# First group of a cross-attention and expert kernel: second scores in the common PSUM banks, beside the next unit's first scores

## The chip, the cores and the metric

The kernel runs on one core of a Trainium2 chip. The metric is device time in microseconds. Engines are named as in the profile: PE (TensorE, matrix products), PEld (its weight loads), DVE (VectorE), ACT (ScalarE), POOL (GpSimd) and SP (SyncE, which issues most loads). PSUM, where PE puts its results, has eight banks of 512 fp32 columns by 128 partitions.

## What is computed

Sixteen images, 100 tokens of width 256 each, attend to 361 context rows with 16 heads of width 16; then a mixture of 16 experts with 64 slots each works on the result. All in fp32.

```python
x = x + xattn(layernorm(x), ctx, mask)     # q, k, v projections, softmax(q k / 4 + mask) v, projection wo
# the experts, per image
xn = layernorm(x1) * norm_g + norm_b
logits   = xn @ se.T                       # 1024 slots, se a layer norm of slot_embeds
dispatch = softmax(logits, over tokens)    # slots = dispatch.T @ xn
combine  = softmax(logits, over slots)
eout     = (gelu(slots @ Wg + bg) * (slots @ Wu + bu)) @ Wd + bd     # per expert
out      = x1 + combine @ eout
```

## The kernel before

The images go in groups of 2, 2, 4, 4 and 4. A group's attention, its dispatch (slots of the experts) and its experts follow each other, and while the experts of one group run, the attention of the next is woven in between. Nothing of that is decided on the chip: while the program is built, a planner (the loop at L1354) keeps a clock for each engine (`Clock`, L64) with an estimated cost for every step, and picks the next step among generators (`Task`, L106). A step says when it can run, how many of four PSUM banks it takes, and what it needs of PE, DVE and ACT. The order in which steps are picked is each engine's order of instructions; on the chip an engine runs its queue in that order, and each instruction waits for its inputs and for its place in memory. Until the first expert step (`begun`), the planner puts *warm products* (L1337, products with the identity that nothing reads) where its clock says that PE would be idle.

PSUM is split in two: four banks are one fixed tile `at` (`at_all`), the other four are a pool that everything else takes in turn (`mm_tile`).

Attention runs in *units*: one image `b`, and four of its heads `cb` (class `Unit`, L769), each head on 32 of the 128 partitions. A unit does, all in `at`:

- `maxima` (L781): first scores, four products of 100 x 361, one bank each (L785), and their negated row maxima by DVE into `mxp` (L790);
- `queries` (L796): the maxima transposed by PE into free columns of `at` (L799) and added to the queries by DVE (L801), so that the second scores come out with the maximum taken off;
- `exponentials` (L805): second scores, transposed, twelve products of 121 x 100 (L810), and one exponential of 1200 columns by ACT (L818);
- `values` (L824): twelve products with the values (L833) into a pool bank, copied by ACT to `cxs` (L842).

`units` (L862) orders them for a group: first scores of a unit, values of the unit before, queries, second scores and exponentials. The first group is images 0 and 1, eight units; unit 4 is the first of image 1.

The side work of the first group: `key_work` (L570: transposed context `c_t` L584, keys `k_ps` L613 with DVE L634 and ACT L639, mask rows by SP L653, values `v_ps` L673 with copies L684 or L687), `query_work` (L491: layer norm with DVE, a power by POOL L447, z L504, `x_t` L519, queries `q_ps` L538 with DVE L548 and ACT L551; L563 adds bo's row to x by POOL), `slot_work` (L451: statistics of `slot_embeds`, its power by POOL, ACT L467, `se_t` L476 and ACT L482), `parameter_work` (L397), `bo_work` (L413: `bo_ps` L423, L426), `out_work` (L701: for each unit a shuffle L713 and a reciprocal L714 by DVE and a product by POOL L717; then `o_ps` L726, the sum L734, the second layer norm, z L747, `xn_t` L752 and ACT L758) and `early_work`. Keys and queries of images 2 and 3, the second group, are side work here too. Then come `dispatch_quarter` (L927: logits L942, DVE L967, ACT L972, `d_t` L1020, slots `sl` L1032) and the experts (L1284, L1244).

While the first group runs, the order of preference among the kinds of side work is a list (`kinds`, L1388), and a step is let in only if by its needs it doesn't keep the next step of the units waiting (`fits`, L1415 on; `lead` holds the steps that must not wait).

Of the kernel before, what the change touches and what calls it, by code (L numbers as in the profile page):

```python
# [33 lines left out]
F32 = mybir.dt.float32  # L34
AF = mybir.ActivationFunctionType
# [9 lines left out]
KC = 120  # L45
# [10 lines left out]
SLACK = 0.6  # L56
BACKLOG = 2.5
ASIDE = ("out_work", "query_work", "key_work")
MASK_DMA = 5.0
COLD = 7.0  # L60
HOP = 0.12
# [68 lines left out]
def xattn_ffn_kernel(  # L130
# [360 lines left out]
    def query_work(b, n=2):  # L491

        g = group_of[b]
        i0 = b - starts[g]
        yield x_t[g], 0, (0.0, 0.65 * n, 0.0)
        mv4 = two.tile([N, 2, 2], F32, tag="mv4", name="mv4")
        for i in range(n):
            ck.run("DVE", stats(accs[g][:, i0 + i, :], N, mv4[:, i, :]), x_t[g])
        r4 = rstd(mv4[:, :n, 1], N, n)
        t = ck.run("POOL", 0.7, ck.run("DVE", 0.15))  # L500
        yield t, 0, (0.0, 0.45 * n, 0.0)
        z4 = const.tile([N, 2, D], F32, tag="z4", name="z4")
        for i in range(n):
            nc.vector.tensor_scalar(  # L504
                z4[:, i, :],
                accs[g][:, i0 + i, :],
                mv4[:, i, 0:1],
                r4[:N, i : i + 1],
                ALU.subtract,
                ALU.mult,  # L510
            )
            t = ck.run("DVE", 0.35, t)
        z_done.add(b)
        yield t, 1, (0.2 * n, 0.0, 0.25 * n)
        xT = const.tile([P, KD, 2 * N], F32, tag="xT", name="xT")
        ps = mm_tile("x_t")
        for kd in range(KD):
            for i in range(n):
                nc.tensor.transpose(  # L519
                    ps[:, (n * kd + i) * N : (n * kd + i + 1) * N],  # L520
                    z4[:, i, kd * P : (kd + 1) * P],
                    ident[:N, :N],
                )
        nc.scalar.copy(
            xT[:, :, : n * N], ps[:, : KD * n * N].rearrange("p (k n) -> p k n", k=KD)
        )
        t = ck.copy(200 * n, ck.run("PE", 0.2 * n, t, ck.bank()))
        ck.free(t)
        yield t, 1, (0.7 * n, 0.5 * n, 0.5 * n)
        if b % 2 == 0:  # L530
            qp = two.tile([P, KD, 2, 2 * N], F32, tag="qp", name="qp")
        else:
            qp = qps[b - 1][0]
        cols = slice(b % 2 * N, (b % 2 + n) * N)
        ps = mm_tile("q_ps")
        for oc in range(KD):
            for kd in range(KD):
                nc.tensor.matmul(  # L538
                    ps[:, oc * n * N : (oc + 1) * n * N],
                    lhsT=w_sb["wq"][:, kd, oc * P : (oc + 1) * P],  # L540
                    rhs=xT[:, kd, : n * N],
                    start=kd == 0,
                    stop=kd == KD - 1,
                )
        t = max(ck.pe(400 * n, t, ck.bank()), par_t[0] if par_t[0] < NEVER else 10.5)
        for oc in range(KD):
            src = ps[:, oc * n * N : (oc + 1) * n * N]
            nc.vector.tensor_scalar(  # L548
                qp[:, oc, 0, cols], src, hm[:, 0:1], qb[:, oc, 0:1], ALU.mult, ALU.add
            )  # L550
            nc.scalar.activation(  # L551
                qp[:, oc, 1, cols], src, AF.Identity, bias=qb[:, oc, 1:2], scale=hm[:, 1:2]
            )
            first = ck.psum_dve(100 * n, t)
            t = ck.copy(100 * n, first)
            if b == oc == 0:
                qps[b] = (qp, first)
        ck.free(t)
        for i in range(n):
            qps.setdefault(b + i, (qp, t))  # L560
        yield (lambda: bo_t[0]), 0, (0.0, 0.0, 0.0)
        a = accs[g][:, i0 : i0 + n, :]
        nc.gpsimd.tensor_tensor(a, a, bo_bc[:N].unsqueeze(1).to_broadcast([N, n, D]), ALU.add)  # L563
        t = ck.run("POOL", 0.55 * n)
        for i in range(n):
            with_bo[b + i] = t
# [202 lines left out]
    class Unit:  # L769
# [35 lines left out]
        def exponentials(self):  # L805
# [15 lines left out]
            if self.cb == 3:  # L821
                live.discard(self.b)

        def values(self):  # L824
            if self.cb == 0:
                live_cxs.add(self.b)
# [18 lines left out]
            cx_t[self.b, self.cb] = t  # L845

    free_t = [0.0]
    phase = [""]
    cx_t = {}
    group_of = {b: g for g, n in enumerate(GROUPS) for b in range(starts[g], starts[g] + n)}  # L850
# [6 lines left out]
    def values_ready(u):  # L857
        if u.b not in values_t or (u.cb == 0 and len(live_cxs) == 2):
            return NEVER
        return max(u.t, values_t[u.b])  # L860

    def units(g):  # L862
        last = None

# [6 lines left out]
                fill.append(Task(key_work(u.b + 2), ck))  # L871

        group = range(starts[g], starts[g] + GROUPS[g])
        for b in group:
            for cb in range(4):
                yield (
                    lambda: max(keys[b, cb][1], qps[b][1]) if (b, cb) in keys and b in qps else NEVER
                ), 0, (0.0, 0.0, 0.0)
                yield free_t[0], 0, (0.8, 1.7, 0.0)
                u = Unit(b, cb)  # L880
                u.maxima()
                if cb == 0 and b % 2 == 1 and b + 1 in group:
                    fill.append(Task(query_work(b + 1), ck))
                if last:
                    lt = last
                    yield (lambda: values_ready(lt)), 1, (0.7, 0.0, 0.3)
                    finish(last)
                yield u.t, 0, (0.15, 0.25, 0.0)
                u.queries()
                yield u.t, 0, (0.85, 0.0, 1.2)  # L890
                u.exponentials()
                last = u
# [461 lines left out]
    while streams["experts"]:  # L1354
# [29 lines left out]
        if waiting:  # L1384
            units_first = dispatches[:WINDOW] + units_first
            side = sorted(fill, key=lambda t: t.kind != "out_work")
            if group == 1 and 0 in qps:
                kinds = (  # L1388
                    "early_work",
                    "bo_work",  # L1390
                    "query_work",
                    "parameter_work",
                    "slot_work",
                    "out_work",
                    "key_work",
                )
                side = sorted(
                    fill,
                    key=lambda t: kinds.index(t.kind) if t.kind in kinds else len(kinds),
                )  # L1400
# [14 lines left out]
        if not begun:  # L1415
# [7 lines left out]
            else:  # L1423
                lead = [
                    i
                    for i, t in enumerate(tasks)
                    if t.kind in ("out_work", "all_experts") or t in dispatches[:1]
                ] if group > 1 else []
            soonest = min((ready[i] for i in lead), default=NEVER)
            by_keys = any(t.kind in ("key_work", "later_keys") and r <= now for t, r in zip(tasks, ready))  # L1430
            for i, t in enumerate(tasks):
# [6 lines left out]
                late = 0.15 + SLACK * pe  # L1438
                if not first_units:
                    fits = max(end, vector, scalar) <= soonest + late  # L1440
                elif phase[0] == "max":
                    fits = max(end, vector) <= soonest + late and scalar <= soonest + late + 1.2
                elif phase[0] != "queries":
# [10 lines left out]
            if ready[-1] <= now:  # L1454
                ready[:-1] = [NEVER] * (len(ready) - 1)
        first = next((i for i, r in enumerate(ready) if r <= now), None)
        if first is None:
            first = min(range(len(ready)), key=lambda i: ready[i])
            assert ready[first] < NEVER
            if not begun and now + 0.2 < ready[first] and phase[0] != "queries":  # L1460
                warm_up()
                continue
        task = tasks[first]
        begun = begun or task is streams["experts"]
        task.step()
        if task.done:
# [63 lines left out]
```

## Time and profile before

| | us |
|---|---|
| median of 3 runs | 1177.96 (1177.79 to 1178.29) |
| span of the profiled execution | 1178.0 |
| PE busy in the span | 1160.2 |
| first unit's first scores | 11.73 |
| last product of the first group's units ends | 64.5 |
| first dispatch logits | 73.0 |
| first expert product | 82.0 |

The span goes from the first to the last instruction of one profiled execution, whose own time with what lies around the span was 1179.8 us. In a timeline line the first two columns are the start and the duration in us, then engine, line, operation, what is written and read, how many in the row, and in brackets how long the engine sat idle before it and what ended that. PE runs an fp32 product as two instructions, so twelve products are a row of 24, and a PE row's duration holds some pipeline time that the next row overlaps; the chain of waits gives such rows without it.

### The profile page before, as it was taken

What the parts mean: (1) busy time and instruction counts of PE and PEld (TensorE: products, weight loads), DVE (VectorE), ACT (ScalarE), POOL (GpSimd) and SP (SyncE); (2) the same over time, 40 slices, a digit from 0 to 9 for tenths busy, and PEclk for the clock granted to TensorE, in tenths of its full rate; (3) what the DMA queues carried; (4) which work ended last, traced back from release to release, by engine and by line L of the source; (5) the groups of instructions that cost most, each with busy time, mean ns of one, the idle gap of its engine ahead of it and who ended that gap; (6) DMA issues with size and microseconds to landing.
All of it is one profiled execution on the core that took longest, in us unless ns stands there. A gap on an engine that the chain in (4) does not pass through costs nothing.

```text
span 1178.0 us, 24309 instructions
## 1 busy us (share of the span) xinstructions
PE 1160.2 (98%) x9825; PEld 899.1 (76%) x9825; DVE 632.8 (54%) x1559; ACT 539.8 (46%) x1112; POOL 150.9 (13%) x255
## 2 busy tenths in 40 slices
PE   8899999999999999999999999999999999999998
PEld 6587778787787777767777776787878878777876
DVE  5755545565654565655386767656543455442222
ACT  3557554664544667434454634646312336314110
POOL 3110301013000131300010010304000003002000
PEclk9999999999999999999999999999999999999999
DMA  4412656543566603212341321333344343345431
GB/s 134 136 38 97 233 174 203 162 145 116 154 201 220 188 11 90 83 58 100 113 105 53 111 91 38 98 126 112 112 158 137 118 148 126 112 129 163 138 131 55
DMA packets 138588, 144.85 MB, mean 123 GB/s; under 512 B 45050, under 2 KB 97228, under 8 KB 138476
## 3 DMA queue, kind: packets, MB, share of 16 engines
q1 hardware_dynamic: 137258, 141.50, 38.6%
q8 instruction: 78, 1.28, 0.4%
q0 software_dynamic: 496, 1.12, 0.3%
q10 hardware_dynamic: 722, 0.67, 0.2%
q14 instruction: 34, 0.28, 0.1%
HBM read 141.60 MB, written 1.66 MB: 122 GB/s over the span
## 4 chain that ended last, share of the span: by engine, by line
PE 94%; DVE 2%; ACT 2%; DMA 1%; issue 1%; POOL 0%; SPq 0%; ACTq 0%; DVEq 0%; POOLq 0%
PE dn L1244 19%; PE gp L1284 19%; PE up L1284 19%; PE sl L1032 5%; PE po L1162 5%; PE at L810 4%; PE at L785 4%; PE lg L942 3%; PE cx L833 3%; PE v_ps L673 3%; PE k_ps L613 3%; PE at L1337 1%; PE o_ps L726 1%; DVE mxp L790 1%; DMA w_all<-in_L_ffn_Wd_dram 1%; PE q_ps L538 1%
## 5 line engine op out<-in xcount | busy, mean ns | idle before, releaser
L1284 PE MATMUL gp<-ring,w_all 128*128 128x256 f32 (+1 forms) x1280 | 247.8, 340 | 1.3 <-ACT lg_all L963 1.3
L1284 PE MATMUL up<-ring,w_all 128*128 128x256 f32 (+1 forms) x1280 | 246.6, 340 | 0.0
L1300 DVE SCALAR_TENSOR_TENSOR hT<-up,parT,ge 128x256 f32<-128x256 f32 (+1 forms) x320 | 119.6, 423 | 233.3 <-PE up L1284 163.0
L1244 PE MATMUL dn<-w_all,hT 128*64 128x256 f32 x2048 | 232.9, 382 | 1.4 <-DMA w_all<-in_L_ffn_Wd_dram 1.3
L1295 ACT ACTIVATE ge<-gp,parT 128x256 f32<-128x256 f32 (+1 forms) x320 | 116.8, 429 | 249.5 <-PE gp L1284 245.3
L1284 PEld LDWEIGHTS gp<-ring,w_all 128*128 128x128 f32 x1280 | 203.4, 191 | 27.5 <-issue 4.9
L1284 PEld LDWEIGHTS up<-ring,w_all 128*128 128x128 f32 x1280 | 203.7, 191 | 21.4 <-issue 1.2
L1244 PEld LDWEIGHTS dn<-w_all,hT 128*64 128x64 f32 x2048 | 142.7, 137 | 79.8 <-issue 8.3
L790 DVE TENSOR_REDUCE mxp<-at 100x4 f32<-100x1444 f32 x64 | 106.2, 1660 | 30.7 <-PE at L785 30.0
L1253 DVE TENSOR_TENSOR ring<-dn,bd_bc 128x512 f32<-128x512 f32 x64 | 44.2, 691 | 136.3 <-PE dn L1244 136.2
L818 ACT ACTIVATE aT<-at 121x1200 f32<-121x1200 f32 x64 | 74.9, 1170 | 64.3 <-PE at L810 60.9
L1295 ACT ACT_TABLE_LOAD x60 | 77.0, 1283 | 26.7 <-PE gp L1284 24.3
L1012 DVE STREAM_TRANSPOSE disp<-d_ex 32x128 f32<-32x128 f32 x256 | 77.4, 302 | 4.5
L717 POOL TENSOR_TENSOR cxs<-cxs,rs 128x100 f32<-128x100 f32 x63 | 24.8, 396 | 390.7 <-DVE rs L714 363.3
L1047 ACT ACTIVATE ring<-sl,parT 128x256 f32<-128x256 f32 x64 | 32.6, 561 | 67.9 <-PE sl L1032 67.9
L1032 PE MATMUL sl<-disp,xn 100*128 100x256 f32 x256 | 63.4, 388 | 0.2 <-ACT disp L1025 0.2
L1162 PE MATMUL po<-ring,lg_all 128*100 128x256 f32 x256 | 60.5, 383 | 0.4 <-DVE ring L1253 0.2
L997 POOL TENSOR_TENSOR d_ex<-d_ex,d_sm 128x400 f32<-128x400 f32 x28 | 23.8, 852 | 267.7 <-DVE d_sm L994 240.6
L810 PEld LDWEIGHTS at<-q,kT 32*121 32x121 f32 x1344 | 40.6, 180 | 19.9 <-issue 8.8
L1032 PEld LDWEIGHTS sl<-disp,xn 100*128 100x128 f32 x256 | 46.4, 190 | 10.3 <-issue 2.6
L810 PE MATMUL at<-q,kT 32*121 32x100 f32 x1344 | 49.9, 277 | 3.4 <-DVE q L801 3.3
L818 ACT ACT_TABLE_LOAD x36 | 46.2, 1283 | 14.2 <-PE at L810 6.2
(152 smaller groups left out, 1268.4 us busy)
## 6 DMA issues: line engine op xcount, KB each, us to landing
w_all<-in_L_ffn_Wg_dram SPq DMA_DIRECT2D x80, 512.0 KB
w_all<-in_L_ffn_Wu_dram SPq DMA_DIRECT2D x80, 512.0 KB
w_all<-in_L_ffn_Wd_dram SPq DMA_DIRECT2D x80, 512.0 KB
bd_bc<-in_L_ffn_bd_dram SPq DMA_DIRECT2D x80, 64.0 KB
c_sb<-in_ctx_dram SPq DMA_DIRECT2D x96, 44.0 KB
acc<-in_x_dram SPq DMA_DIRECT2D x7, 200.0 KB
out_dram<-acc SPq DMA_DIRECT2D x7, 200.0 KB
ring<-n_L_ffn_slot_embeds_dram POOLq DMA_DIRECT2D x1, 1024.0 KB, 6.6
```

Source lines behind the costliest of these rows:

```text
L785: nc.tensor.matmul(self.at[:N, r, :S2], lhsT=self.q[rows], rhs=self.k[rows], start=True, stop=True)
L790: nc.vector.tensor_reduce(mxv[:, :, m : m + 1], self.at[:N, :, :S2], AX.X, ALU.max, negate=True)
L810: nc.tensor.matmul(self.at[: KC + 1, r, c * N : (c + 1) * N], lhsT=self.k[rows, c * KC : c * KC + KC + 1], rhs=self.q2[rows], start=True, ...
L818: nc.scalar.activation(self.aT[: KC + 1], self.at[: KC + 1, :, : 3 * N], AF.Exp)
L1012: nc.vector.transpose(dst[toks, :, :, a, :], src[32 * a : 32 * a + 32, :, :, toks])
L1032: nc.tensor.matmul(sl[:, kd * 256 : (kd + 1) * 256], lhsT=xns[g][:, b0 + i, kd * P : (kd + 1) * P], rhs=disp[:, i, :], start=True, stop=True,)
L1162: nc.tensor.matmul(pos[i][:N, :D], lhsT=lg_all[:, slot, 2 * c + i, :], rhs=eouts_of(g, q)[:, c, 2 * p + i, :], start=c == 0, stop=c == 1,)
L1244: nc.tensor.matmul(dn[S * x : S * x + S, i * D : (i + 1) * D], lhsT=hts[x][fc // FB][0].rearrange("p (f b s) -> p f b s", f=FB, s=S)[:, fc ...
L1253: nc.vector.tensor_tensor(eouts_of(g, q)[:, j // 2, 2 * half : 2 * half + 2, :], dn.rearrange("p (b d) -> p b d", d=D), biases[k // 2].uns ...
L1284: nc.tensor.matmul(ps[:, f * T : (f + 1) * T], lhsT=w[:, kd, fc * P : (fc + 1) * P], rhs=slots_of(g, q)[:, j, kd].rearrange("p b s -> p (b ...
L1295: nc.scalar.activation(ge[:, cols], ps[:, cols], AF.Gelu, bias=col(8, e, fc))
L1300: nc.vector.scalar_tensor_tensor(out=hT[:, cols], in0=ps[:, cols], scalar=col(NPAR, e, fc), in1=ge[:, cols], op0=ALU.add, op1=ALU.mult,)
```

## The change

For group 0 `units` now hands over to a new generator, `first_units`. Second scores no longer lie in `at`: `half_exponentials` takes two pool banks for two heads, makes their six products and two exponentials of 300 columns, one a head; a unit does so twice. So the next unit's first scores can go to `at` as soon as the sum with the transposed maxima has read it, and `first_units` puts them there: queries of unit n, first scores of unit n+1, values of unit n-1, second scores of unit n in halves. The other groups run as before.

The rest is in the planner. `query_work` counts DVE and ACT on the query projection as parallel. The list of kinds has keys and queries first. Output, slot, bo and parameter steps are let in while they fit in an allowance `spare`, which each unit's first scores set to 0.7 us and which each such step lowers. A DVE-only step of `slot_work` or `out_work` is put in at once when DVE would be idle within 0.15 us. `slot_work` joins the leads after the first group.

In the order that results, the first expert product comes after the same steps as before, but for the key and value products of image 3 (`k_ps` and `v_ps`), which now follow it. There are 53 warm products before it in both. Those that follow a unit's first scores, or its transpose, in PE's queue wait for DVE's reduction, or sum.

```diff
+SPARE = 0.7
+IDLE = 0.15
@@ query_work
-        t = max(ck.pe(400 * n, t, ck.bank()), par_t[0] if par_t[0] < NEVER else 10.5)
+        tm = max(ck.pe(400 * n, t, ck.bank()), par_t[0] if par_t[0] < NEVER else 10.5)
...
-            first = ck.psum_dve(100 * n, t)
-            t = ck.copy(100 * n, first)
+            first = ck.psum_dve(100 * n, tm)
+            t = max(first, ck.copy(100 * n, tm))
@@ class Unit
+        def half_exponentials(self, half):
+            if half == 0:
+                self.aT = two.tile([P, 4, 3 * N], F32, tag="aT", name="aT")
+                self.parts = []
+            ps = [mm_tile(f"sc{r}") for r in range(2)]
+            t = max(ck.bank(), ck.bank())
+            for c in range(3):
+                for r in range(2):
+                    rows = slice(32 * (2 * half + r), 32 * (2 * half + r) + 32)
+                    nc.tensor.matmul(
+                        ps[r][: KC + 1, c * N : (c + 1) * N],
+                        lhsT=self.k[rows, c * KC : c * KC + KC + 1],
+                        rhs=self.q2[rows],
+                        start=True,
+                        stop=True,
+                    )
+            tp = ck.run("PE", 0.55, self.t, t)
+            for r in range(2):
+                nc.scalar.activation(
+                    self.aT[: KC + 1, 2 * half + r], ps[r][: KC + 1, : 3 * N], AF.Exp
+                )
+                t = ck.act("exp", 290, tp)
+                ck.free(t)
+            self.parts.append(t)
+            if half == 1:
+                self.t = t
+                if self.cb == 3:
+                    live.discard(self.b)
@@ after values_ready
+    def first_units(finish, group):
+        held = before = None
+        nexts = [(b, cb) for b in group for cb in range(4)] + [None, None]
+        def there(n):
+            b, cb = n
+            return (b, cb) in keys and b in qps
+        def scores(n):
+            b, cb = n
+            yield (
+                lambda: max(keys[b, cb][1], qps[b][1]) if there(n) else NEVER
+            ), 0, (0.0, 0.0, 0.0)
+            yield free_t[0], 0, (0.8, 1.7, 0.0)
+            u = Unit(b, cb)
+            u.maxima()
+            free_t[0] = u.t
+            spare[0] = SPARE
+            made.append(u)
+        made = []
+        for n in nexts:
+            if held:
+                yield held.t, 0, (0.15, 0.25, 0.0)
+                held.queries()
+                phase[0] = "max"
+            if n and there(n):
+                yield from scores(n)
+            if before:
+                lt = before
+                yield (lambda: values_ready(lt)), 1, (0.7, 0.0, 0.3)
+                finish(before)
+                before = None
+            if held:
+                for half in range(2):
+                    yield held.t, 2, (0.5, 0.0, 0.9)
+                    held.half_exponentials(half)
+                before = held
+            if n and not made:
+                if before:
+                    lt = before
+                    yield (lambda: values_ready(lt)), 1, (0.7, 0.0, 0.3)
+                    finish(before)
+                    before = None
+                yield from scores(n)
+            held = made.pop() if made else None
@@ units
+        if g == 0:
+            yield from first_units(finish, group)
+            return
@@ the planner's loop
                 kinds = (
+                    "key_work",
+                    "query_work",
+                    "bo_work",
+                    "parameter_work",
+                    "out_work",
+                    "slot_work",
                     "early_work",
-                    "bo_work",
-                    "query_work",
-                    "parameter_work",
-                    "slot_work",
-                    "out_work",
-                    "key_work",
                 )
...
-                    if t.kind in ("out_work", "all_experts") or t in dispatches[:1]
+                    if t.kind in ("out_work", "slot_work", "all_experts") or t in dispatches[:1]
...
+                elif t.kind in ("slot_work", "out_work", "bo_work", "parameter_work"):
+                    fits = ready[i] <= now and max(pe, dve, act) <= spare[0]
                 elif phase[0] == "max":
...
+        if not begun and ck.t["DVE"] <= now + IDLE:
+            for i, t in enumerate(tasks):
+                alone = t.needs[0] == 0 and t.needs[1] > 0
+                if alone and t.kind in ("slot_work", "out_work") and t.ready() <= now:
+                    first = i
+                    break
...
         task = tasks[first]
+        if task.kind in ("slot_work", "out_work", "bo_work", "parameter_work"):
+            spare[0] -= max(task.needs)
```

More of the change, by code (lines that the diff above doesn't have):

```diff
@@ L847, in xattn_ffn_kernel @@
     free_t = [0.0]
+    spare = [0.0]
     phase = [""]
```

## The prediction, made before the changed kernel was run

> **What bounds the kernel now.** I read the page's busy rows and chain first, then the table of windows, then the timeline of one unit of the first group, then the chain of waits by stage.
>
> ```profile
> PE 1160.2 (98%) x9825; PEld 899.1 (76%) x9825; DVE 632.8 (54%) x1559; ACT 539.8 (46%) x1112; POOL 150.9 (13%) x255
> ...
> PE 94%; DVE 2%; ACT 2%; DMA 1%; issue 1%; POOL 0%; SPq 0%; ACTq 0%; DVEq 0%; POOLq 0%
> ```
>
> TensorE is the bound: work taken off another engine counts only where TensorE waits or runs warm products (L1337), which compute nothing. The windows say where that is:
>
> ```profile
> 11.70:64.60 52.90, 46.63 (x592) 31.63 (x592) 35.63 (x81) 27.19 (x49) 9.45 (x24) 1.00 0.41 119
> 64.60:82.00 17.40, 17.40 (x109) 15.13 (x110) 9.74 (x27) 7.66 (x22) 3.18 (x6) 1.00 0.01 3
> 82.00:100.00 18.00, 16.66 (x135) 14.91 (x135) 10.05 (x23) 14.90 (x43) 0.00 (x0) 1.00 0.25 89
> 100.00:200.00 100.00, 100.00 (x1086) 80.98 (x1085) 51.56 (x134) 53.71 (x100) 12.62 (x21) 1.00 0.59 194
> ```
>
> Columns: window, length, then busy us of PE, weight loads, DVE, ACT, POOL, then clock. The first group's units run from 11.7 to 64.6, their tail to the first expert product at 82.0; after 100 TensorE is full. In the first 82 us TensorE runs 53 warm products, some 0.24 us each (11 pairs cost 2.46 us in the chain), and idles 7.6 us before L1337 and L810. One unit:
>
> ```profile
> 57.66 0.87 PE L785 MATMUL at<-kT,qp 32*100 32x361 f32 x8
> ...
> 58.66 1.66 DVE L790 TENSOR_REDUCE mxp<-at 100x4 f32<-100x1444 f32 x1 [1.14 <-PE at L785]
> ...
> 60.38 0.49 PE L1337 MATMUL at<-ident 128*128 128x128 f32 x2 [0.16 <-DVE mxp L790]
> ...
> 60.70 0.25 PE L799 MATMUL at<-ident,mxp 100*128 100x100 f32 x1
> 60.99 0.26 DVE L801 TENSOR_TENSOR q<-at,qp 128x100 f32<-128x100 f32 x1 [0.32 <-PE at L799]
> ...
> 61.31 0.89 PE L810 MATMUL at<-q,kT 32*121 32x100 f32 x24 [0.35 <-DVE q L801]
> ...
> 62.31 1.17 ACT L818 ACTIVATE aT<-at 121x1200 f32<-121x1200 f32 x1 [2.83 <-PE at L810]
> ```
>
> First scores, reduction 1.0 us later, transpose, sum, second scores, exponentials: one tile `at` holds all of it, so the next first scores wait for the exponentials (31.21 to 31.26 in another unit). First scores start at 11.73, 17.54, 25.00, 31.26, 37.66, 44.35, 51.27 and 57.66. A warm product also writes `at`: at 60.38 it starts only when the reduction has ended.
>
> **What it removes.** From the loop: 0.96 us from second scores to exponentials, 1.17 us of exponentials, 0.05 us. Left is 1.00 (to the reduction) + 1.66 + 0.06 + 0.34 (transpose to sum) + 0.32 (sum to the next first scores) = 3.4 us instead of about 5.6. The number of products, and of warm products (53), stays; 96 second-score products only change tile. The edits of the planner (its clock in query_work, SPARE, IDLE, the list of kinds, slot_work among the leads) issue nothing: they act through the order alone, which the walk below follows.
>
> **What it adds in the loop.** (a) Four exponentials of 300 columns for one of 1200. L842's copy (100 columns, 0.24) and L818 (1200, 1.17) bound one at 0.24 and 0.47; I take 0.40, so +0.43 us a unit on ScalarE, hidden: it is busy 27 of 53 us. (b) A half's 12 products use two row groups where L810 uses four. The 24 records of L810 took 0.89 us, six to a group. If the pace is that of issue, a half costs 0.41 (two halves as before); if it is that of a group, 0.82. Full-array records of 100 columns (L538, eight in 0.97) take 0.12 each, as a group's do, so I take 0.73: 1.45 a unit, +0.6, of which about 1.3 us in all lies where TensorE sets the pace (ends 0 and +2). (c) Work now stands in VectorE's queue between reduction and sum. Three times it is a shuffle and a reciprocal (0.26 + 0.78): 1.05 less the 0.40 that the transpose takes anyway, +0.65 each.
>
> The Trainium skill, "TensorEngine Tiling (Array Packing)", section "Theoretical Speedup", gives four-fold speed to contractions of 32 rows, for four tiles at once; with two in use a half would cost as much as a whole of L810 did, by estimate 0.82, or 1.64 a unit. The rule speaks against the change; going by it the sum would be 0.5 us higher (0.19 a unit, where two to three units count), going by the row's pace of issue 1.3 us lower. No row of this profile has two groups alone.
>
> **The walk by instruction order.** Starts of first scores, from the order of the changed kernel and these rows:
> - 16.7, 20.6, 24.6 for units 1 to 3 (4 us apart: 3.4 + 0.65): the gain is 6.7 us by unit 3.
> - Unit 4 needs image 1's keys, values and queries, which now all follow unit 3's first scores. TensorE: first scores 0.84, parameters 0.25, three value products (L833) 1.98, two units of second scores 2.9, two key products (L613) 2.44, three L673 2.64, L538 0.97, c_t 0.62, a warm product 0.24, a bank wait 0.4: 13.3. Unit 4 starts at 38.0; before 37.66. The lead is gone.
> - Units 5, 6, 7: reduction 4 waits 0.5 for L436 statistics; then 8 and 3 warm products wait for reductions 4 and 5 and so stand wholly in the loop (1.9, 0.7), and unit 7 has a reciprocal before it: 43.8, 47.9, 51.9. Before: 57.66 for the last, a lead of 5.7.
> - Unit 7's sum, though, stands behind a statistics step and its wait for GpSimd: 0.6 + 0.15 + 1.7 + 0.2 after the reduction (54.6), so it ends at 57.7 instead of 55.3. Queued behind it on TensorE are five warm products (they wait for the sum, 1.2), then value products 6 (0.66), second scores 7 (1.45), a key product (1.22), value products 7: these end at 63.0, before at 64.5.
>
> The price of that wait is in these rows:
>
> ```profile
> 42.30 1.68 POOL L447 TENSOR_TENSOR rstd<-rstd,neghalf 128x8 f32<-128x8 f32 x1
> ```
>
> **Tail.** Before, the first dispatch logits (L942) start at 73.0, 8.5 after the last unit. Now bo's product, both o_ps, all se_t and both layer norms come after it: VectorE has L634 0.65, a shuffle and reciprocal 1.05, bo_bc 0.42, another 1.05, product and sum 0.5, L734 0.42, norm 0.75 with a GpSimd step 0.54, L734 again, L747 0.40, norm again, 0.73 (z), 0.65 (keys), L747: about 9 us, with ScalarE's L639 and eight L467 beside it. Logits at 73.4; the 9.0 us from there to the first expert product stay (same steps). So the experts start at 82.4, **+0.4**.
>
> **What is put off.** Image 3's keys and values, done before 82.0 now, stand after the first expert product: 2 x 1.22 + 3 x 0.88 = **+5.1 us** of TensorE work that filled no gap. In SP's queue image 3's four mask loads (L653) still follow image 4's context loads; what moves is the two loads of x (L184), now ahead of image 2's second pair of masks, 0.94 us of issue that no unit waits for so early. On POOL the power of the slots now comes before the two additions of bo (L563, 1.40), which the tail below its first wait already counts.
>
> **Opening of the experts.** Before, TensorE waits 1.34 us at 90.39 for a bank that the third logits hold until ScalarE has copied them. Now a key product wants that bank at 88.4 (2.0 us), and the next dispatch waits 0.75 for ScalarE, which has key work ahead of the copy: **+1.4**.
>
> **Sum.** 0.4 + 5.1 + 1.4 = +6.9. The profiled run's span is 1178.0 us, the median of the runs 1177.96, so they agree: **1184.8 us**. Later waits of TensorE in the trace after 100 us come to 4.6 (DMA 1.3; 1.0, 1.0, 0.6 and small ones); the order there changes too, and I carry them over, with 0 and twice as bounds (-4.6, +4.6).
>
> The clock: granted 1.00 throughout, with waits up to 1.34 us; the longest new one, before the warm products of unit 4, is 2.2 us. I count no loss. The Trainium skill, "TensorE: Matmul & The Clock Gate", section "What's actually happening", puts the idle time that halves the clock at about 3.4 us, longer than this wait; no run here shows it.
>
> **Rivals.**
> 1. *The lead lives.* Unit 7's start is 5.7 us early; if the sum of unit 7 isn't held by GpSimd and the tail keeps its 24.35 us (57.66 to 82.01), experts start at 76.3: -5.7 + 5.1 (put off), and the put-off key work fills the 1.34 wait and 0.4 beside it: -2.3, **1175.6**; with half of the later waits gone, 1173.3. For it: the engines have room in the first 82 us. Against: the order puts the GpSimd wait ahead of the sum. It decides if second scores 7 start before 57.
> 2. *A draw.* Halves cost 0.41 (-1.3), the tail is as short as before with its own start (8.5 for 10.4: -1.9), the opening waits are no longer than before (-1.4): +2.3, **1180.3**, or less if a later wait goes. For it: three separate estimates of mine are each the dearer end. Against: the 5.1 us put off remain.
> 3. *Later waits double*: **1189.4**, the new order meeting loads (the 9.9 us weight load on the chain near 353) at worse moments.
>
> **Chances.** Forecast and rival 3 together 0.70 (0.58 and 0.12), the draw 0.17, the lead 0.13. A measurement here tells 0.2% (2.4 us) from no change; so faster 0.13, same 0.17, slower 0.70. Range 1175.5 to 1190: it takes in the lead's own time and rival 3, leaving out the tails of both. The forecast's own range is 1181 to 1188.
>
> **What will show it.** Unit 4's first scores near 38 and unit 7's near 52; GpSimd's 128x8 power between the last reduction and its sum; warm products that start when a reduction or sum ends; halves of 0.7 us; logits near 73.4 and the first expert product near 82.4, followed by image 3's keys; a wait of 2 us at the second of these. Wrong if the first expert product comes before 79, or if TensorE's time after 100 us differs by more than 3 us beyond image 3's work.

## The result and the profile after

| | before | after |
|---|---|---|
| median of 4 runs each, us | 1178.12 (1177.79 to 1179.66) | 1192.06 (1191.44 to 1194.56) |
| ratio of after to before | | 1.0123, interval 1.0111 to 1.0136 |
| profiled execution: span, us | 1178.0 | 1189.9 |
| first expert product starts, us | 82.17 | 85.22 |

The change made the kernel slower by 14 us, twice the 6.9 us forecast and 2 us above the top of the range. The first expert product is here the product itself; the 82.0 us given for the kernel before is the start of its weight load (82.01). The busy rows, the row of the granted clock (40 slices of 30 us) and the chain of the kernel after:

```profile
PE 1166.8 (98%) x9825; PEld 906.1 (76%) x9825; DVE 633.8 (53%) x1564; ACT 541.8 (46%) x1133; POOL 151.2 (13%) x255
...
PEclk9899999999999999999999999999999999999999
...
PE 90%; DVE 4%; ACT 3%; DMA 2%; issue 1%; SPq 1%; POOL 0%; ACTq 0%; DVEq 0%; POOLq 0%
```

PE has the same 9825 instructions as before and is busy 6.6 us longer with them. The second digit of the clock is an 8, and DVE has 4% of the chain where it had 2%. The table of windows, first by stage as before, then by 5 us:

```profile
11.70:64.60 52.90, 44.23 (x535) 32.97 (x528) 30.69 (x70) 19.58 (x56) 8.11 (x22) 0.90 0.34 102
64.60:82.00 17.40, 16.94 (x130) 14.40 (x129) 10.86 (x30) 12.69 (x32) 4.49 (x8) 1.00 0.20 44
82.00:100.00 18.00, 15.70 (x92) 13.10 (x91) 9.12 (x19) 12.86 (x35) 0.00 (x0) 1.00 0.12 25
...
50.00:55.00 5.00, 2.44 (x31) 1.51 (x34) 3.18 (x6) 0.89 (x3) 1.08 (x2) 0.76 0.02 3
55.00:60.00 5.00, 4.64 (x45) 3.93 (x38) 2.18 (x8) 1.60 (x5) 1.39 (x2) 0.50 0.00 0
60.00:65.00 5.00, 4.71 (x56) 3.42 (x54) 0.35 (x2) 1.60 (x5) 0.70 (x1) 0.72 0.00 0
...
52.50:53.00 0.50, 0.00 (x0) 0.00 (x0) 0.50 (x1) 0.00 (x0) 0.00 (x0) 0.57 0.00 0
...
62.50:63.00 0.50, 0.50 (x18) 0.50 (x16) 0.00 (x0) 0.00 (x0) 0.00 (x0) 0.69 0.00 0
```

From 52.57 to 62.81 us PE is granted half its clock (the last two windows hold the two changes); before, it had 1.00 up to its last product. The timeline at its start, unit 7:

```profile
50.88 0.87 PE L787 MATMUL at<-kT,qp 32*100 32x361 f32 x8 [0.78 <-DVE q L803]
51.82 1.66 DVE L792 TENSOR_REDUCE mxp<-at 100x4 f32<-100x1444 f32 x1 [0.99 <-PE at L787]
...
53.53 0.80 PE L1423 MATMUL at<-ident 128*128 128x128 f32 x2 [1.78 <-DVE mxp L792]
...
54.31 1.68 POOL L449 TENSOR_TENSOR rstd<-rstd,neghalf 128x8 f32<-128x8 f32 x1 [3.06 <-DVE rstd L448]
...
55.42 2.07 PE L836 MATMUL sc<-q,kT 32*121 32x100 f32 x24
...
57.43 0.43 PE L801 MATMUL at<-ident,mxp 100*128 100x100 f32 x1
57.89 0.26 DVE L803 TENSOR_TENSOR q<-at,qp 128x100 f32<-128x100 f32 x1 [1.70 <-PE at L801]
```

PE waits 0.78 us for a sum, runs first scores, and then waits 1.78 us with a single warm product (L1423, two records) that needs the reduction. Behind it, second scores take 2.0 us. The last line is the one to read with care: GpSimd's power ended at 55.99, but the sum waited for the transposition by PE, which stood behind the slow products.

First scores started at 16.15, 19.96, 23.72, 37.48, 43.09, 47.11 and 50.88, each within 1.1 us of the walk; logits came at 76.09 (forecast 73.4). Behind the first expert product, these windows (columns as before) show the other part of the loss. Before, then after:

```profile
82.17:1178.00 1095.83, 1085.70 (x9073) 843.15 (x9072) 581.26 (x1420) 501.28 (x1035) 130.54 (x198) 1.00 0.40 124
```

```profile
85.22:1189.90 1104.68, 1092.41 (x9093) 847.35 (x9092) 584.45 (x1428) 504.64 (x1036) 130.75 (x198) 1.00 0.40 123
```

There are 20 PE records more, which are image 3's keys (8) and values (12). The stretch is 8.85 us longer: 6.7 of PE busy and 2.1 of PE idle (length less busy time: 10.13 and 12.27). The longest wait there is in front of image 3's keys, for a bank:

```profile
93.43 1.48 PE L615 MATMUL k_ps<-cT,wk 128*128 128x361 f32 x4 [1.91 <-ACT lg_all L1049]
```

So 11.9 us of span = 3.05 ahead of the first expert product + 8.85 behind it.

### The profile page after: what moved, and what is told of

Its sections match the earlier page's. It is cut to its first block, busy times and chain, and to the rows that moved or that the text cites. A ratio compares the mean times of both kernels' runs of the same rounds, so it can differ in the third digit from the quotient of the medians.

```text
span 1189.9 us, 24326 instructions
## 1 busy us (share of the span) xinstructions
PE 1166.8 (98%) x9825; PEld 906.1 (76%) x9825; DVE 633.8 (53%) x1564; ACT 541.8 (46%) x1133; POOL 151.2 (13%) x255
## 4 chain that ended last, share of the span: by engine, by line
PE 90%; DVE 4%; ACT 3%; DMA 2%; issue 1%; SPq 1%; POOL 0%; ACTq 0%; DVEq 0%; POOLq 0%
PE dn L1330 19%; PE gp L1370 19%; PE up L1370 18%; PE sl L1118 5%; PE po L1248 4%; PE at L787 4%; PE at L812 4%; PE cx L865 3%; PE lg L1028 3%; PE v_ps L675 2%; PE k_ps L615 2%; DMA w_all<-in_L_ffn_Wd_dram 1%; DVE mxp L792 1%; PE o_ps L728 1%; PE at L1423 1%
## 5 line engine op out<-in xcount | busy, mean ns | idle before, releaser
L820 ACT ACTIVATE aT<-at 121x1200 f32<-121x1200 f32 x56 | 65.5, 1170 | 49.9 <-PE at L812 49.0
L874 ACT COPY cxs<-cx 128x100 f32<-128x100 f32 x64 | 15.5, 242 | 89.8 <-PE cx L865 85.6
L1248 PEld LDWEIGHTS po<-ring,lg_all 128*100 128x100 f32 x256 | 41.5, 167 | 13.9 <-issue 1.8
```

What stands on the lines that cost most here:

```text
L820: nc.scalar.activation(self.aT[: KC + 1], self.at[: KC + 1, :, : 3 * N], AF.Exp)
L1248: nc.tensor.matmul(pos[i][:N, :D], lhsT=lg_all[:, slot, 2 * c + i, :], rhs=eouts_of(g, q)[:, c, 2 * p + i, :], start=c == 0, stop=c == 1,)
```

## The experiments

Three theories. **A, the clock**: PE stands idle too much of the time at some place of the loop and is granted half its clock for some 10 us. **B, the chain**: warm products that wait for reductions, and the sum behind GpSimd, hold the loop. **C, put off**: image 3's work behind the first expert product, and the waits that come with it. No experiment leaves out or changes a part of the computation. Each gave this, with the start of the first expert product and the length behind it from its profile:

| run | median, us | ratio (interval) | clock of profile | first expert product | behind it |
|---|---|---|---|---|---|
| x1_drop_one_warm | 1192.67 | 1.0121 (1.0099 to 1.0143) | 0.995 | 85.70 | 1104.5 |
| x2_power_after_sum | 1193.97 | 1.0132 (1.0117 to 1.0148) | 0.994 | 85.80 | 1105.6 |
| x3_both | 1186.47 | 1.0084 (1.0053 to 1.0114) | 0.990 | 87.94 | 1104.9 |
| x4_four_at_once | 1194.11 | 1.0132 (1.0117 to 1.0147) | 0.994 | 87.78 | 1103.9 |
| x5_warm_beside | 1184.75 | 1.0052 (1.0037 to 1.0067) | 0.998 | 76.70 | 1106.3 |
| x6_warm_beside_power_after | 1183.98 | 1.0058 (1.0037 to 1.0079) | 1.000 | 76.56 | 1104.2 |
| x7_units_alone | 1199.77 | 1.0181 (1.0163 to 1.0199) | 0.993 | 91.18 | 1104.3 |
| x8_rules_alone | 1186.81 | 1.0077 (1.0046 to 1.0107) | 0.998 | 88.80 | 1093.2 |
| x9_room_for_keys | 1178.23 | 0.9998 (0.9990 to 1.0007) | 1.000 | 80.20 | 1096.3 |
| x10_more_room | 1195.32 | 1.0142 (1.0128 to 1.0155) | 0.993 | 87.88 | 1105.4 |
| x11_before_put_off | 1187.63 | 1.0073 (1.0060 to 1.0087) | 0.997 | 81.80 | 1105.0 |
| x12_filled_waits | 1189.80 | 1.0105 (1.0088 to 1.0121) | 1.000 | 81.73 | 1105.4 |

### One or six warm products left out, the power later (x1, x2, x3)

The warm product between unit 7's first scores and unit 5's values is number 30 (from 0), the five behind unit 7's transposition are 31 to 35.

```diff
+    LEFT_OUT = [30]      # x1; x3: [30, 31, 32, 33, 34, 35]
...
     def warm_product():
+        warmed[0] += 1
+        if warmed[0] - 1 in LEFT_OUT:
+            return
```

x2, and x3 with it, move the power of `slot_work` and the two DVE steps around it behind the next sum:

```diff
-        r = rstd(mv[:, :, 1], P, ES // P)
...
+        def power():
+            r = rstd(mv[:, :, 1], P, ES // P)
...
+        after_sum.append(power)
...
             nc.vector.tensor_tensor(self.q2, tp, self.q, ALU.add)
+            while after_sum:
+                after_sum.pop()()
```

> The changed kernel (1192.06 us) without one warm product, the one in TensorE's queue between unit 7's first scores and unit 5's value products; it waits 1.78 us for the reduction there, and holds back value products and second scores that could run. Theory A (the clock): TensorE ran too little from 49.9 to 53.5, so its clock fell to half from 52.8 to 62.6, which cost 4 to 5 us; without the wait the clock stays at 1.00 all through, and the time falls by 4 to 6 us, to about 1187. Rival B (the chain): the loss is unit 7's sum behind GpSimd's power and the five warm products after it; the clock only stretches work that waits anyway; then at most 1.5 us. Rival C (work put off): what sets the end is image 3's products after the first expert product; no change.

> The changed kernel with GpSimd's 128x8 power and the two VectorE steps around it put behind unit 7's sum instead of ahead of it; nothing else moves. A: the clock still falls near 52.8, since the 1.78 us wait before it stays; the sum comes about 2.6 us earlier (after its transpose), but TensorE at half rate is still busy with unit 5's values and unit 6's second scores until 57.5, so the gain is under 1 us. B: the sum comes 2 to 2.6 us earlier and so does all behind it: 1189.5. C: no change.

> Both at once, and without the five warm products that wait for unit 7's sum. A and B together: clock 1.00, second scores 7 start near 55 instead of 61.8, first expert product near 79 to 80 instead of 85.2, time about 1185 (-7). If A alone holds: -5. If C holds: the first expert product comes earlier and the end doesn't.

Neither x1 nor x2 alone gained; x3 gained 5.6 us by the medians. But within one kernel the time went with the granted clock: x3's executions took 1185.4 to 1186.5 us at a mean clock of 0.998 and 1194.5 and 1194.6 at 0.988 and 0.990; x1's took 1189.4 at 0.998, 1192.0 at 0.995, 1195.8 at 0.991. That is some 0.9 us for each 0.001. In x1 the drop of the clock only moved, to 56.1 to 66.4 us. These runs could not part A from B: they changed where PE idles together with what it waits for.

### Second scores over four row groups at once (x4)

All 24 records of a unit are issued together, over four banks, as in the kernel before.

```diff
-            for c in range(3):
-                for r in range(2):
-                    rows = slice(32 * (2 * half + r), 32 * (2 * half + r) + 32)
...
+            for c in range(3 * half):
+                for r in range(4):
+                    rows = slice(32 * r, 32 * r + 32)
...
+            for r in range(4 * half):
+                nc.scalar.activation(
+                    self.aT[: KC + 1, r], ps[r][: KC + 1, : 3 * N], AF.Exp
+                )
```

> The changed kernel with a unit's 24 second-score records issued as the kernel before issued them, four row groups in turn, into the four common banks, and the four exponentials after them. The trace has 1.24 us for a unit's two halves in a row against 0.82 for L810 before. If those 0.4 us a unit count in full, -3.3 us (1188.8); if they are hidden in half of the units, -1.5; the exponentials of the first half start later, which gives back up to 0.4 us a unit where the values wait for them. The clock should still fall.

No gain. The first unit's 24 records took 0.79 us by their row, for 1.08 in the kernel after and 0.89 before, and unit 4's 0.82 for 1.11; units 1, 2 and 5 took 1.30 (1.23 to the start of the next row), as long as two halves in a row. In this profile the clock dropped in two places (41.48 to 44.89 and 55.13 to 65.37 us). So nothing that can be measured hung on the pace of the halves.

### Warm products beside the loop (x5), and the power later as well (x6)

The 20 warm products from number 16 on (groups of 2, 1, 8, 3, 1 and 5; the expectation says 21) write a pool bank that nobody reads, so they wait for no reduction or sum. The order of every engine stays.

```diff
+    beside = [None]
+
     def mm_tile(name):
+        beside[0] = None
...
     def warm_product():
+        warmed[0] += 1
+        if 16 <= warmed[0] - 1 <= 35:
+            beside[0] = beside[0] or ps_mm.tile([P, 512], F32, tag="mm", name="warm")
+            for _ in range({}.get(warmed[0] - 1, 1)):
+                nc.tensor.matmul(beside[0][:, :P], lhsT=ident, rhs=ident, start=True, stop=True)
+            return
         nc.tensor.matmul(at_all[:, 3, 384:], lhsT=ident, rhs=ident, start=True, stop=True)
```

> The 21 warm products from the one behind unit 2's first scores to the five before unit 7's values write a bank of the pools, no longer the tile that the reduction reads; the order on every engine is that of the changed kernel. Theory A (the clock: TensorE runs thinly behind these waits for 2 to 3 us and is then granted half its clock): no window of the first 66 us below 0.9, mean clock 0.998 or above in most runs, and the time falls by the 4.5 us that the clock costs and by some 2 us of waits, to 1184 to 1187. Theory B (the chain: products that wait for reductions and the sum, whatever the clock): the warm products start with no wait, unit 7's first scores come at 48.5 to 49.5 instead of 50.9, but a drop stays, 1189 to 1190. Theory C (put off and later waits alone): the first expert product may come 2 to 3 us earlier, yet the time stays above 1190.

> As the run with the warm products beside the loop, and the power of the layer norm and its two steps on VectorE behind unit 7's sum. Theory A: clock 0.998 or above, and within 1 us of the run with the warm products alone (1184 to 1187). Theory B: the sum, which no longer stands behind the wait for GpSimd, and the products behind it come 2 to 3 us earlier than in that run, and so does the first expert product: 2 us less than it. Theory C: no difference between the two, both above 1190.

The timeline of x5 at unit 7:

```profile
48.22 0.87 PE L790 MATMUL at<-kT,qp 32*100 32x361 f32 x8 [0.78 <-DVE q L806]
49.01 0.49 PE L1432 MATMUL warm<-ident 128*128 128x128 f32 x2
49.43 0.72 PE L868 MATMUL cx<-aT,vpad 120*32 120x100 f32 x24
50.09 1.30 PE L839 MATMUL sc<-q,kT 32*121 32x100 f32 x24
```

The 1.78 us wait is gone, first scores 7 start 2.7 us earlier than after, the clock is 1.00 up to 86 us, and the first expert product comes at 76.70. (Behind it, from 86.47 to 89.88 us, the clock did fall, after a wait of 1.91 us for a bank; in x6's profile it didn't, and the stretch is 2.1 us shorter.) Moving the power as well gave 0.14 us there and nothing in the time: the intervals of x5 and x6 lie on each other. So of theory B the warm products hold, and GpSimd falls. But x6's lead of 5.6 us on the kernel before still ends in a loss of some 5 us.

### The waits filled, nothing else (x12)

This parts A from the chain: 17 more warm products in a pool bank, ahead of the ones that wait. They wait for no reduction or sum (the second group waits 0.23 us for its bank), and first scores 4 and 7 both come 0.3 us later than after, so the 11 extra products between them delayed nothing.

```diff
+    EXTRA = {19: 8, 27: 3, 30: 6}
+
     def warm_product():
         warmed[0] += 1
+        for i in range(EXTRA.get(warmed[0] - 1, 0)):
+            beside[0] = beside[0] or ps_mm.tile([P, 512], F32, tag="mm", name="warm")
+            nc.tensor.matmul(beside[0][:, :P], lhsT=ident, rhs=ident, start=True, stop=True)
```

> The changed kernel with 17 more warm products (8, 3 and 6) in a bank of the pools, each set right ahead of the warm products that wait for reductions 4, 5 and 7: they fill the waits of 2.21, 0.87 and 1.78 us with products that wait for nothing, and every wait's end stays where it is. All else is the changed kernel. Theory A (the clock falls because TensorE runs thinly there): no window of the first 66 us below 0.9, mean clock 0.998 or above, 1187 to 1188 in spite of 17 more products; the products behind the last wait take their normal length, so the first expert product comes 3 to 5 us earlier. Theory B (the chain alone): the chain is untouched, so 1191 to 1193. Theory C: 1191 to 1193 too.

```profile
51.20 0.86 PE L790 MATMUL at<-kT,qp 32*100 32x361 f32 x8 [0.78 <-DVE q L806]
51.99 1.60 PE L1432 MATMUL warm<-ident 128*128 128x128 f32 x12
53.85 0.49 PE L1433 MATMUL at<-ident 128*128 128x128 f32 x2 [0.25 <-DVE mxp L795]
54.27 0.72 PE L868 MATMUL cx<-aT,vpad 120*32 120x100 f32 x24
54.92 1.30 PE L839 MATMUL sc<-q,kT 32*121 32x100 f32 x24
```

The wait for the reduction ends where it did (53.85, 0.3 later like first scores 7), but the products behind it take their normal length: second scores 1.24 us for 2.0. The clock was 0.999 or 1.000 in all four executions. The first expert product came 3.5 us earlier than after, as A expected; the time fell by 2.3, to 1189.8, where A expected 1187 to 1188. So idle time on PE brought the drop, and filling it held the clock; which of the three waits had to be filled was not tested apart. A is real, and in the end smaller than its rival C (2.3 us for the 5.8 of x9 below).

### The two halves of the change by themselves (x7, x8)

x7 has the new units with the former planner rules; x8 the former units with the new rules, SPARE set at each unit's maxima.

> The new order of the first group's units and their halves of second scores, with the former rules for the side work (list of kinds, clock of query_work, leads, no SPARE, no IDLE). Image 3's keys and values stand behind the first expert product as in the changed kernel, 19 warm products more are run one behind another at three places. Theory A: 0.50 in some window of the first 66 us or not, time 0.9 us per 0.001 of mean clock above 1186 to 1188. Theory C: the 5.1 us of image 3's keys and values and later waits are lost here too, so at full clock 1184 to 1188, never the time of the kernel before. A rival, that the side work's new rules make the loss: 1178 to 1180.

> The former order of the units (second scores in the tile of the first scores) with the new rules for the side work. Image 3's keys and values stand ahead of the first expert product, as in the kernel before. Theory C: nothing is put off, so within 2 us of the kernel before, 1176 to 1180, with the first expert product at 81 to 84. Theory A: clock 1.00 as before, since first scores wait for exponentials as before and no run of warm products waits for a reduction longer than before; same time. The rival, that the new rules make the loss: 1184 or more.

x7 is 7.7 us slower than the whole change by the medians, at a clock of 0.988 to 0.993. The 0.9 us for each 0.001 does not explain all of it: some 3 to 5 us are left over the 1186 to 1188 expected at full clock, and the first expert product is 6 us later. The new rules help the new units. x8 missed my expectation of the same time as before, and lies where the rival had it (1184 or more). Behind the first expert product it loses nothing (1093.2, image 3's work is ahead of it), but that product comes at 88.80. The same new rules hold up the former units; two lines of its timeline:

```profile
35.10 0.89 PE L812 MATMUL at<-q,kT 32*121 32x100 f32 x24 [1.60 <-DVE q L803]
...
42.60 1.38 PE L1421 MATMUL at<-ident 128*128 128x128 f32 x10 [1.21 <-DVE mxp L792]
```

The sum, and the reduction, come late; the first of these waits was 0.36 us in the kernel before. So the rules cost time with the former units and save some with the new ones; the two halves of the change do not add up to the whole. The clock fell here too (0.70 in the window from 35 to 40 us).

### Image 3's work put off in the kernel before (x11), and put back in the new one (x9, x10)

```diff
     def later_keys(b):
+        if b == 3:
+            yield (lambda: 0.0 if begun else NEVER), 0, (0.0, 0.0, 0.0)
         yield from key_work(b)
```

> The kernel before, with image 3's keys and values held back until the first expert product is issued; its tail has 22 warm products more in their place and all work there keeps its steps. Theory C: the first expert product comes at 80 to 82, as before or a little earlier, and the time is that of the kernel before plus 4 to 6 us: 1182 to 1184. Rival (the 5.1 us fit into waits of the expert stage, or are won by an earlier first expert product): within 2 us of 1178.

x11's first expert product came at 81.80, 0.4 us earlier than before, and the stretch behind it was 9.2 us longer. The time rose by 9.5, to 1187.63, more than the 4 to 6 I expected. Two things are in it that I hadn't counted. The edit puts off 30 PE records, not the 20 that the change does: image 3's transposed context (6) and a transposition of x (4) go with its keys and values. And a new wait of 2.47 us ahead of image 3's transposition (L584) came with a drop of the clock of its own, from 88.76 to 95.59 us (0.81 in the window from 82 to 100); half a clock for 6.8 us is 3.4 us, by estimate, which leaves some 6.

x9 is x6 with SLACK 1.0 for 0.6 and SPARE 1.2 for 0.7, so that the planner lets image 2's keys into the loop, and image 3's keys and values come ahead of the first expert product; x10 has SLACK 2.5.

> The run with warm products beside the loop and the power behind the sum, with SLACK 1.0 for 0.6 and SPARE 1.2 for 0.7: the side work that it lets in is image 2's and 3's keys and values, 40 warm products for 53, and image 3's keys and values all ahead of the first expert product. Theory C (put off: some 6 us of TensorE work behind the first expert product is what keeps a lead of 5.5 us there from reaching the end): the first expert product comes at 76 to 80 with nothing put off, and the time is 1173 to 1178 at full clock. Rival (the order behind the first expert product costs the rest whatever was put off): 1181 or more, though the first expert product comes before 80. Theory A: below 0.998 of mean clock, 0.9 us more for each 0.001.

> The same with SLACK 2.5: image 2's keys move into the loop (units 4 and 5), image 3's stand between the last units and the first expert product, 43 warm products. Theory C: nothing put off, so 1173 to 1179 at full clock; side work that is allowed to be late by more may hold up the units, so that the first expert product comes at 78 to 82. Rival (order behind the first expert product): 1181 or more.

The windows of x9, ahead of and behind its first expert product:

```profile
0.00:80.20 80.20, 73.83 (x728) 56.41 (x729) 50.18 (x139) 39.45 (x101) 20.44 (x57) 1.00 0.37 106
80.20:1176.50 1096.30, 1085.44 (x9073) 843.10 (x9072) 582.91 (x1422) 506.77 (x1037) 130.96 (x198) 1.00 0.40 124
```

9073 records again, and 1085.44 us of PE as before. With the clock held and nothing put off, the new units give 1178.23 us against 1178.08, no difference that can be measured: x9 has taken back the loss (I had expected 1173 to 1178), but beats nothing. It spends 3.6 us of x6's lead on the work that x6 puts off, and that work cost x6 7.9 us behind the first expert product (1104.2 less 1096.3).

x10 shows that letting more in is no remedy. Its tail has a wait of 2.83 us and a first drop of the clock; behind the first expert product there is one from 239.1 to 242.5 us, and one at 407 us, by these two lines, of the timeline and of the windows:

```profile
407.10 2.74 PE L628 MATMUL k_ps<-cT,wk 128*128 128x361 f32 x4 [3.66 <-DVE d_sm L1095]
...
400.00:410.00 10.00, 6.34 (x25) 4.45 (x24) 7.19 (x20) 3.88 (x18) 2.82 (x4) 0.82 0.32 110
```

Nothing is put off in x10, and still the stretch behind is 1105.4 long, where I had expected 1173 to 1179 in all: of the 9.1 us over x9's stretch 4.4 are PE busy, with two drops of the clock, and the rest is PE idle. So theory C is not the whole rule. Image 3's work put off is enough for such a loss (x11), and putting it back took the loss away in x9, but another order behind the first expert product can cost as much, as the rival said.

By the medians the way from the kernel after to x9 is 13.8 us: 7.3 for the warm products out of the tile (x5; filling the waits alone gave 2.3, x12), 0.8 that the intervals do not tell from nothing (x6), and 5.8 for image 3's work (x9).

## Why the prediction was wrong, point by point

The direction and the shape of the loss were right: slower, with image 3's work as the largest part. The step that failed is "The clock: granted 1.00 throughout, with waits up to 1.34 us; the longest new one, before the warm products of unit 4, is 2.2 us. I count no loss."

- **The clock, 0 forecast, +3.5 us at the first expert product** (85.22 after, 81.73 with the waits filled; 2.3 in the medians). I had looked for the longest wait alone. That one, 2.21 us, came as foreseen and did nothing in the profiled execution. The clock fell at unit 7, where two waits of 0.78 and 1.78 us stand close to each other. The walk names the 8, 3 and 5 warm products and not the single one behind unit 7's first scores, which makes the wait of 1.78; and I did not ask how much PE idles over a few us. The Trainium skill, which I cited, agrees only in part: "TensorE: Matmul & The Clock Gate", section "What's actually happening", has the throttle come back after an idle window of about 3.4 us. Here PE was busy for 1.82 of the 3.42 us before the drop, and the drop came 0.8 us into a wait of 1.78. The measurement decides.
- **First expert product at full clock, +0.4 forecast, -0.4 measured** (x12). The walk holds. That the 8 and 3 warm products "stand wholly in the loop", and the 5 behind the sum, holds too, and moving them and four others aside was worth 5.0 us there (81.73 to 76.70).
- **Unit 7's sum behind GpSimd, wrong.** At half clock the sum waited for PE's transposition; at full clock in x12 the transposition ended at 56.46 and the sum started at 56.50, right behind GpSimd's step, so GpSimd held it for 0.05 us at most; and with the warm products beside the loop taking the power away gave 0.14 us. The order put it ahead of the sum, but I took its place in the queue for its price.
- **Put off, +5.1 forecast, +6.7 of PE busy measured; opening, +1.4 forecast, +1.0 measured; later waits, carried over, some +1.2.** The bank wait was 1.91 (forecast 2.0) and the one behind it 0.39 (forecast 0.75), less the 1.34 before. PE idle rose by 2.1 in all, so the rest lies in small waits later on, which I have not traced. The groups of keys and values account for 6.1 us by their busy sums, in which rows overlap; where the other 0.6 lies I have not traced either. Together 8.85 for 6.5.
- **Halves of the second scores, 1.45 forecast for two in a row, 1.23 measured; one alone 0.81** against 0.73. Near enough, and x4 shows no gain from a faster issue.
- **The base.** "The profiled run's span is 1178.0 us, the median of the runs 1177.96, so they agree" sets a span beside a time. The profiled execution's own time was 1179.8, 1.7 above the median of the runs in the table (1178.12), and why it was longer is not known. From that, and 0.4 the other way in the kernel after, the medians differ by 2 us more than the two profiles.

Sum: -0.4 + 3.5 + 8.85 = 11.9 in the profiles for 6.9. Rival 1, the lead that lives, fell in an instructive way: its lead was there in x6 (76.56 for its 76.3), and the time was still 1184.0 and not 1175.6, because the work put off found no wait to fill. Rival 2's dearer ends were not the cause. Rival 3 came nearest in time (1189.4) for another reason: PE's waits behind the first expert product rose by 2.1 us, not by 4.6.

What stays open: whether a planner could place image 3's work in the loop so as to keep more of the lead than the 2 us by which x9's first expert product is early. x9 and x10 are two settings only.

## What to carry to other kernels

A lead that comes from leaving work for later is no gain where the bounding engine is full later: count the records behind the point at which it becomes full, before and after. Where the clock is granted, ask not only how long the longest wait is but how much the engine works in any 3.4 us around it: in these traces under 1.5 us of PE work in such a step always brought half a clock, and under 2.2 sometimes. Filling such waits with products that wait for no result cost nothing that could be seen here, if they write memory that nobody reads. A filler that writes the tile being worked on inherits every wait of that tile.

## What the runs showed of the hardware that was not expected

- PE's granted clock fell to 0.50 at 52.57 us, 0.8 us into a wait of 1.78 us, with PE busy for 1.82 us of the 3.42 before. In the same execution a wait of 2.21 us, at unit 4, brought no drop. In x3 and x4 the same wait of 2.21 us did.
- In each profiled execution every change of the clock lay a whole number of steps of 3.41 us from every other. The kernel after had half a clock from 52.57 to 62.81 us (three steps); x4 from 41.48 to 44.89 (one) and from 55.13 to 65.37 (three), three steps apart; x7 from 25.14 to 35.38 (three), from 66.10 to 69.52 and from 100.24 to 103.65 (one each), nine steps apart both times; the other drops lasted one, two, three or six steps. Where these steps begin differs between executions, so one wait may fall into one step or be split over two: the wait at unit 4 left PE busy for 1.21 us of a step in x3 (38.15 to 41.57), and for 1.78 of the step in the kernel after in which it ended (38.91 to 42.33). Over all the traces, each step at full clock with less than 1.5 us of PE work was followed by half a clock, none with more than 2.2 was, and of those between eight of some thirty were. What else decides there was not found. That the steps lie differently may be why executions of one kernel differ (1185.4 to 1194.6 us in x3); it is not shown, as one execution of each kernel was profiled.
- Once down, the clock came back at 62.81 us, after three steps in which PE was busy for 2.44, 3.06 and 3.41 us. In x5, where PE worked throughout the first step at half clock, it came back after that one (86.47 to 89.88). In all traces a step before a return had at least 3.1 us of PE work. The Trainium skill, "TensorE: Matmul & The Clock Gate", section "What's actually happening", has the throttle released after some 3.4 us of sustained work; these traces agree in the size, though in x7 a step with PE busy throughout (28.56 to 31.97) brought no return. Half a clock for 10.24 us is 5 us, of which 3.5 reached the first expert product.
- The 24 records of second scores took 0.89 us in the kernel before and 0.79 and 0.82 in units 0 and 4 of x4, over four row groups; and 1.30 in units 1, 2 and 5 both of the kernel after (two row groups at a time) and of x4 (four); what sets the 1.30 was not measured.
